# Moving the half-column products of a two-layer graph kernel next to its 64-unit tiles, on one Trainium2 core

## The chip, the cores and the metric

The kernel runs on one core of a Trainium2 chip. The metric is the device time of one launch in microseconds (us), as the median of several executions. A second kind of number comes from one profiled execution, in which the hardware records every instruction; its time is told beside the timed ones.

The engines are named as in the profile: PE is TensorE (matrix products; PEld its weight loads), DVE is VectorE, ACT is ScalarE, POOL is GpSimd, SP is the engine whose queue issues nearly all DMAs. Each works through its own instructions in order and waits on semaphores for the others.

## The reference

There are 128 graphs of 128 nodes with 64 features. Layer 0 sums, for each node j, a small network over its neighbours k (those with `adj > 0`); layer 1 is a weighted sum over neighbours and a linear map. Both are applied to a normalised, rectified x and added to x:

```
h = max(layernorm(x), 0)
A = h @ W1a + h @ W1b + b1          # per node j; W1 is (128, 192): two halves of 64 rows
C = h @ W1b                         # per node k
hm[j] = sum over k with adj[j,k] > 0 of relu(A[j] - C[k])      # 192 hidden units
x1 = x + hm @ W2 + deg * b2         # W2 is (192, 64)
h2 = max(layernorm(x1), 0)
out = x1 + (adj @ h2) @ W.T
```

Everything is float32 in and out. A node has some 15 neighbours, so the kernel does not evaluate all 128 x 128 pairs.

## The kernel before, in words

**Groups.** The 128 graphs are taken in 32 groups of four (`G = 4`). A group's neighbours are put into slots: each node's neighbours are ranked within four quarters of the nodes, six slots to a quarter (`D = 6`), and the rare rest goes through "edges" (`et`, `R`, `S2`, `X`). `S` is a one-hot matrix of slots, computed on VectorE; `ca` holds the projections A and C split into three bfloat16 parts. `S` and `ca` are restacked by DMA into `S3` and `k3` (12 DMAs each, all on SP's queue, lines 442 to 640), so that one product with 96 rows picks a slot's neighbour exactly and a second adds the node's own part.

**Jobs.** A group's main work is 24 jobs (`Job`, line 818). Each fills a two-bank PSUM tile, of which there are three (`gtile`), and drains it. Hidden units 0 to 127 are one kind: products that use all 128 columns of TensorE, drained by a VectorE reduction (`hm<-g`). Hidden units 128 to 191 are the other: 64 units, so two graphs share a tile, each with 64 of TensorE's columns (shapes `96*64` in the profile), drained by a ScalarE activation into `T` and additions on GpSimd. I call the second kind 64-unit jobs. `ORDER` (line 920) puts them in runs of two: positions 4 and 5, 10 and 11, 16 and 17, 22 and 23 of 24.

**Pieces.** Between the jobs stand pieces of work for other groups. While group g's jobs run, `AHEAD` (line 890) prepares group g+1 and `BEHIND` (line 909) finishes group g-1; a key t means "after job t", and at one t the order is `OWN`, `BEHIND`, `AHEAD` (`pieces`, line 927). The pieces that matter here, with their tiles in PSUM (two small ones, `mtile`, used in turn):

- `pre_adj`, `pre_norm`, `pre_hT` (tiles `pt`, `ph`): transposes of adjacency and of normalised x, and the neighbour mask `maskT`.
- `pre_rank` (line 442, tile `pq`): the ranks, one product with 512 columns, copied by ScalarE to `qs`; VectorE makes `ov` and then the slots `S` from it (`pre_slots`).
- `pre_count` (tile `pd`), `pre_proj` (tiles `pp`, of the large kind), `pre_stack` (the DMAs of `k3`), `pre_edge_a` (line 623, tile `pv`; VectorE makes `mid`, ScalarE the first `et`), `pre_edge_b`, `pre_place`, `pre_edge_c`, `pre_edge_d` (tiles `pj`, `prt`, `pgq`).
- `edge_sum` (tile `pe0`) and `edge_sum1` (line 731, tile `pe1`): the edges' part for the first 128 and the last 64 units. In the profile both are called `pe`. VectorE makes `u0` and `u1` from them. `pe1` is two all-column transposes and then four half-column products.
- `post0` (line 751, tile `py`): y = u W2, as two half-column products with `u0` (`w2h`) and one all-column product with `u1` (`w2bd`), added up in PSUM; ScalarE copies it to `ys`.
- `post1` (line 772, tile `pty`): transposes of `ys` back; VectorE adds to `x1` and takes the statistics. `post2`: a square root on ScalarE (`sdb`), two small VectorE operations (`rsb`, `mrb`), then four ScalarE activations `h2` (in the profile `h<-x,mrb,rsb`). `post3` (line 791, tile `pga`): four half-column products with `h2`; `post4` (tile `po`): the last linear map, and the store.

**What sets the order.** TensorE's instructions keep the order in which the program writes them (`mm`, line 180). The other engines' orders within the main loop are free: a planner in the tile layer decides them when the kernel is built, and which PSUM buffer a tile gets. So a piece that is moved can change the order on VectorE, ScalarE and GpSimd well beyond its own place.

Group 0 and the last group have orders of their own (`ORDER0`, `ORDERL`); after the last group its `BEHIND` pieces run alone.

Of the kernel before, what the change touches and what calls it, by code (L numbers as in the profile page):

```python
# [150 lines left out]
def kernel(  # L151
# [28 lines left out]
    def mm(*args, **kw):  # L180
        return tc.keep_in_program_order(nc.tensor.matmul(*args, **kw))  # L181
# [23 lines left out]
    B, N, F = x.shape  # L205
# [22 lines left out]
    with ExitStack() as main:  # L228
# [11 lines left out]
        def mtile(name):  # L240
            return ps_m.tile([P, 512], F32, tag="m", name=name)
# [7 lines left out]
        w2bd = const.tile([P, 2, O], F32, tag="w2bd", name="w2bd")  # L249
# [134 lines left out]
        def bc(t, n, axis):  # L384
            shape = list(t.shape)
            shape.insert(axis, n)
            return t.unsqueeze(axis).to_broadcast(shape)
# [67 lines left out]
        def pre_slots(g, first, last):  # L455

            d = groups[g]
            if first == 0:
                d["S"] = one.tile([P, D, G * N], BF16, tag="S", name=f"S{g}")
            n = last - first  # L460
            vec.tensor_tensor(
                d["S"][:, first:last], bc(d["qs"].rearrange("k b j -> k (b j)"), n, 1),
                rks[:, first:last], ALU.is_equal,
            )
            if last < D:
                return
            d["S3"] = grp.tile([K3, Q, D, G * N], BF16, tag="S3", name=f"S3{g}")
            for q in range(Q):
                for part in range(3):
                    sp.dma_start(  # L470
                        d["S3"][part * QN : (part + 1) * QN, q],
                        d["S"][q * QN : (q + 1) * QN],
                    )
# [277 lines left out]
        def post0(g):  # L751
            d = groups[g]
            py = mtile(f"py{g}")
            d["py"] = py
            for p in range(2):
                s = slice(p * O, (p + 1) * O)
                mm(
                    py[s, 0 : 2 * N], w2h,
                    d["u0"][:, 2 * p : 2 * p + 2].rearrange("h r j -> h (r j)"),
                    start=True, stop=False, skip_group_check=True,  # L760
                )
            w = w2bd.rearrange("h p o -> h (p o)")
            mm(
                py[:, 0 : 2 * N], w, d["u1"].rearrange("h r j -> h (r j)"),
                start=False, stop=True, skip_group_check=True,
            )
            d["ys"] = tmp.tile([P, 2, N], F32, tag="ys", name=f"ys{g}", bufs=1)
            act.activation(
                d["ys"].rearrange("p r j -> p (r j)"), py[:, 0 : 2 * N], AF.Copy
            )  # L770
# [47 lines left out]
        class Job:  # L818
# [70 lines left out]

        AHEAD = {  # L890
            0: (pre_adj,),
            2: (pre_norm, pre_hT,),
            3: (pre_rank, lambda g: pre_slots(g, 0, 2),),
            4: (lambda g: pre_slots(g, 2, 4),),
            5: (pre_count,),
            6: (lambda g: pre_slots(g, 4, D),),
            7: (lambda g: pre_proj(g, 0),),
            9: (pre_edge_a,),
            12: (lambda g: pre_proj(g, 1), pre_stack,),
            19: (pre_edge_b,),  # L900
            20: (pre_place,),
# [7 lines left out]
        BEHIND = {  # L909
            0: (slot_sum,),  # L910
            1: (edge_sum,),
            4: (edge_sum1,),
            8: (post0,),
            10: (post1,),
            15: (post2,),
            16: (post3,),
            19: (post4,),
        }

# [114 lines left out]
```

## Time and profile before

| | before |
|---|---|
| timed executions | 993.23, 994.23, 1002.85 us, median 994.23 |
| profiled execution | 1005.13 us |
| its span, first to last instruction | 1003.4 us |
| mean granted TensorE clock | 0.978 |
| busy: PE, DVE, ACT, POOL | 94%, 80%, 70%, 76% |
| VectorE's waits for TensorE (`hm` for `g`) | 113.2 us, 113 times |
| TensorE's waits for `k<-ca` | 18.5 us, 22 times, the longest 7.2 |
| TensorE's waits for `hm` | 15.2 us, 31 times |

The profiled execution was slower than two of the three timed ones, so differences are formed within the profile and then set against the median. The busy share of PE counts pipelined products by modelled ends; where products follow each other closely, the distance between their starts is the better measure of what each costs. A group's mean in the table of costliest groups mixes shapes where it says "+2 forms". The waits name the instruction that released a wait; a wait that hides behind another engine's longer one costs nothing.

### The profile page before, as it was taken

What the parts mean: (1) busy time and instruction counts of PE and PEld (TensorE: products, weight loads), DVE (VectorE), ACT (ScalarE), POOL (GpSimd) and SP (SyncE); (2) the same over time, 40 slices, a digit from 0 to 9 for tenths busy, and PEclk for the clock granted to TensorE, in tenths of its full rate; (3) what the DMA queues carried; (4) which work ended last, traced back from release to release, by engine and by line L of the source; (5) the groups of instructions that cost most, each with busy time, mean ns of one, the idle gap of its engine ahead of it and who ended that gap; (6) DMA issues with size and microseconds to landing.
All of it is one profiled execution on the core that took longest, in us unless ns stands there. A gap on an engine that the chain in (4) does not pass through costs nothing.

```text
span 1003.4 us, 26630 instructions
## 1 busy us (share of the span) xinstructions
PE 947.9 (94%) x9994; PEld 695.8 (69%) x9994; DVE 801.2 (80%) x1769; ACT 706.3 (70%) x1732; POOL 767.5 (76%) x1134
## 2 busy tenths in 40 slices
PE   3899999999999999999999999999999999999996
PEld 2577776677776777777677767677767777777674
DVE  7677888877888878788887787887888887788863
ACT  5557876667877767787677785677787677787652
POOL 3287877787877878877788786778877788787783
PEclk9599999999999999999999999999999999999997
DMA  3626665556766555766555765555766655665520
GB/s 87 134 69 160 153 139 131 127 121 150 157 138 139 129 122 136 164 143 142 126 125 126 159 148 123 124 126 136 164 141 138 134 127 124 157 148 127 111 60 13
DMA packets 88293, 129.89 MB, mean 129 GB/s; under 512 B 47200, under 2 KB 63968, under 8 KB 88160
## 3 DMA queue, kind: packets, MB, share of 16 engines
q1 hardware_dynamic: 87584, 127.98, 56.4%
q8 instruction: 80, 1.31, 0.5%
q14 instruction: 53, 0.43, 0.1%
q10 hardware_dynamic: 576, 0.16, 0.1%
HBM read 13.01 MB, written 4.19 MB: 17 GB/s over the span
## 4 chain that ended last, share of the span: by engine, by line
PE 37%; DVE 23%; ACT 19%; DMA 7%; POOL 6%; issue 4%; SPq 3%; DVEq 0%; POOLq 0%; ACTq 0%
PE g L181 21%; DVE hm L198 7%; DVE S L198 7%; PE pe L181 7%; DMA k<-ca 6%; ACT ca L198 5%; ACT et L198 4%; POOL T L198 4%; SPq L198 3%; ACT h L198 3%; ACT T L198 3%; DVE u L198 3%; POOL ca L198 2%; ACT z L198 2%; PE px L181 2%
## 5 line engine op out<-in xcount | busy, mean ns | idle before, releaser
L198 POOL TENSOR_TENSOR T<-T 128x192 f32<-128x192 f32 (+2 forms) x768 | 545.7, 717 | 124.3 <-ACT T L198 84.4
L198 DVE TENSOR_REDUCE hm<-g 128x64 f32<-128x768 f32 x512 | 473.4, 950 | 117.0 <-PE g L181 113.2
L181 PEld LDWEIGHTS <-k 96*128 96x128 bf16 (+1 forms) x6144 | 412.8, 104 | 213.9 <-issue 87.0
L181 PE MATMUL g<-S,k 96*128 96x384 bf16 (+1 forms) x2048 | 392.5, 333 | 34.9 <-DMA k<-ca 18.5
L181 PE MATMUL g<-id,k 96*128 96x192 bf16 (+1 forms) x4096 | 383.9, 248 | 0.0
L198 ACT ACTIVATE T<-g 128x768 f32<-128x768 f32 x256 | 210.2, 823 | 51.7 <-PE g L181 45.7
L198 POOL TENSOR_TENSOR ca<-rest,ca 128x384 bf16<-128x384 f32 x126 | 113.9, 924 | 85.3 <-ACT ca L198 83.6
L198 ACT ACTIVATE ca<-pp 128x768 bf16<-128x768 f32 x64 | 51.4, 804 | 63.7 <-PE pp L181 63.7
L198 DVE TENSOR_TENSOR S<-qs,rks 128x1024 bf16<-128x1024 bf16 x93 | 86.8, 934 | 0.0
L198 ACT ACTIVATE hT<-ph 128x256 f32<-128x256 f32 x32 | 12.3, 384 | 89.4 <-PE ph L184 89.4
L181 PE MATMUL pe<-RT,X 128*64 128x128 f32 (+1 forms) x512 | 71.3, 282 | 0.0
L181 PE MATMUL pp<-wp,hT 64*128 64x448 f32 x256 | 68.5, 613 | 0.0
L198 ACT ACTIVATE z<-pp,ns 128x128 f32<-128x128 f32 (+1 forms) x256 | 66.0, 348 | 0.0
L198 DVE TENSOR_TENSOR rest<-pp,ca 128x768 f32<-128x768 f32 x64 | 60.7, 949 | 3.0 <-ACT ca L198 2.8
L198 ACT ACTIVATE ca<-rest 128x768 bf16<-128x768 f32 x64 | 55.2, 862 | 9.3 <-DVE rest L198 9.2
L181 PEld LDWEIGHTS pe<-RT,X 128*64 128x64 f32 (+1 forms) x512 | 53.4, 166 | 5.3 <-issue 5.3
L198 ACT ACTIVATE et<-et,half 128x128 f32<-128x128 f32 x128 | 56.8, 449 | 0.0
L181 PE MATMUL px<-ca,S 128*128 128x192 bf16 x384 | 52.7, 246 | 0.0
L181 PE MATMUL px<-ca,R 128*128 128x192 bf16 x384 | 52.6, 246 | 0.0
L198 ACT ACTIVATE h<-x,mrb,rsb 128x64 f32<-128x64 f32 x128 | 51.6, 479 | 0.8 <-DVE mrb L198 0.8
L181 PE MATMUL pe<-ident,z 128*128 128x128 f32 x192 | 49.9, 287 | 0.0
L198 ACT ACTIVATE h<-x,mra,rsa 128x64 f32<-128x64 f32 x128 | 48.7, 432 | 1.1 <-DVE mra L198 1.1
(128 smaller groups left out, 1203.9 us busy)
## 6 DMA issues: line engine op xcount, KB each, us to landing
S<-S SPq DMA_DIRECT2D x372, 192.0 KB, 4.0
k<-ca SPq DMA_DIRECT2D x384, 96.0 KB, 2.2
adj<-in_adj_dram SPq DMA_DIRECT2D x32, 256.0 KB, 3.1
x<-in_x_dram SPq DMA_DIRECT2D x32, 128.0 KB, 2.7
out_dram<-ot SPq DMA_DIRECT2D x32, 128.0 KB, 2.2
w<-in_L_gnn_W_dram SPq DMA_DIRECT2D x2, 96.0 KB, 4.4
bias<-in_L_gnn_b_dram ACTq DMA_DIRECT2D x1, 96.0 KB, 3.8
w2a<-in_L_gnn_W_dram ACTq DMA_DIRECT2D x1, 32.0 KB, 2.1
```

The lines of the kernel that those rows point to most:

```text
L181: return tc.keep_in_program_order(nc.tensor.matmul(*args, **kw))
L198: ins = f(*args, **kw)
```

## The change

Four pieces move to an earlier place (`edge_sum1`, `pre_rank`, `pre_edge_a`, `post2`), three to a later one (`post0`, `post1`, `post3`), and the products of `post0` change their order: the all-column product opens the sum in PSUM, and the two half-column products close it. The pieces' arithmetic is otherwise the same. After the change, `edge_sum1` ends in its half-column products directly before job 4, `post0` in its own directly before job 10, `post3` stands directly behind job 17, and nothing stands between the two jobs of any run.

```
         def post0(g):
...
-            for p in range(2):
-                s = slice(p * O, (p + 1) * O)
-                mm(
-                    py[s, 0 : 2 * N], w2h,
-                    d["u0"][:, 2 * p : 2 * p + 2].rearrange("h r j -> h (r j)"),
-                    start=True, stop=False, skip_group_check=True,
-                )
             w = w2bd.rearrange("h p o -> h (p o)")
             mm(
                 py[:, 0 : 2 * N], w, d["u1"].rearrange("h r j -> h (r j)"),
-                start=False, stop=True, skip_group_check=True,
-            )
+                start=True, stop=False, skip_group_check=True,
+            )
+            for p in range(2):
+                s = slice(p * O, (p + 1) * O)
+                mm(
+                    py[s, 0 : 2 * N], w2h,
+                    d["u0"][:, 2 * p : 2 * p + 2].rearrange("h r j -> h (r j)"),
+                    start=False, stop=True, skip_group_check=True,
+                )
...
         AHEAD = {
             0: (pre_adj,),
-            2: (pre_norm, pre_hT,),
-            3: (pre_rank, lambda g: pre_slots(g, 0, 2),),
+            2: (pre_norm, pre_hT, pre_rank),
+            3: (lambda g: pre_slots(g, 0, 2),),
...
-            9: (pre_edge_a,),
+            8: (pre_edge_a,),
...
         BEHIND = {
             0: (slot_sum,),
             1: (edge_sum,),
-            4: (edge_sum1,),
-            8: (post0,),
-            10: (post1,),
-            15: (post2,),
-            16: (post3,),
+            3: (edge_sum1,),
+            9: (post0,),
+            13: (post1,),
+            14: (post2,),
+            17: (post3,),
             19: (post4,),
         }
```

More of the change, by code (lines that the diff above doesn't have):

```diff
@@ L754, in post0 @@
             d["py"] = py
+            w = w2bd.rearrange("h p o -> h (p o)")
+            mm(
+                py[:, 0 : 2 * N], w, d["u1"].rearrange("h r j -> h (r j)"),
+                start=True, stop=False, skip_group_check=True,
+            )
             for p in range(2):
@@ L759, in post0 @@
                     d["u0"][:, 2 * p : 2 * p + 2].rearrange("h r j -> h (r j)"),
-                    start=True, stop=False, skip_group_check=True,
+                    start=False, stop=True, skip_group_check=True,
                 )
-            w = w2bd.rearrange("h p o -> h (p o)")
-            mm(
-                py[:, 0 : 2 * N], w, d["u1"].rearrange("h r j -> h (r j)"),
-                start=False, stop=True, skip_group_check=True,
-            )
             d["ys"] = tmp.tile([P, 2, N], F32, tag="ys", name=f"ys{g}", bufs=1)
```

## The prediction

> **What bounds the kernel now.** I read the busy shares first, then the waits, then one group of four graphs instruction by instruction: group 9 of the 32, from the end of its `pe0` products (394.91 us) to the end of the next group's (425.05 us). All clock times below are this group's unless I say otherwise.
>
> ```profile
> PE 947.9 (94%) x9994; PEld 695.8 (69%) x9994; DVE 801.2 (80%) x1769; ACT 706.3 (70%) x1732; POOL 767.5 (76%) x1134
> ```
>
> TensorE looks like the only bound, but a share is an average. In the stretches the picture is different; first TensorE's timeline (start, length, what, and in brackets the idle time and who ended it):
>
> ```profile
> 396.36 0.39 PE L181 MATMUL pq<-maskT,triq 128*128 128x512 bf16 x1
> ...
> 397.02 0.50 PE L181 MATMUL g<-id,k 96*64 96x192 bf16 x8
> 397.45 0.44 PE L181 MATMUL pe<-ident,z 128*128 128x128 f32 x2
> 397.82 0.66 PE L181 MATMUL pe<-RT,X 128*64 128x128 f32 x8
> ...
> 402.36 0.48 PE L181 MATMUL g<-S,k 96*128 96x384 bf16 x2 [0.55 <-DVE hm L198]
> ...
> 413.19 0.50 PE L181 MATMUL g<-id,k 96*64 96x192 bf16 x8
> 413.52 0.61 PE L181 MATMUL pga<-adjT,h 128*64 128x128 f32 x8
> ...
> 421.04 0.32 PE L181 MATMUL g<-S,k 96*128 96x384 bf16 x1 [0.22 <-DMA k<-ca]
> ```
>
> Two things are to be seen. First the price of changing between half columns (the `96*64`, `128*64` shapes) and all columns (`128*128`): the same eight half-column products take 397.02 to 397.45, 0.43 us, when all-column work follows, and 413.19 to 413.52, 0.33 us, when half-column work (`pga`) follows. One change costs 0.10 us (0.095 between single records, in all 30 groups). Second, TensorE stands still twice in the group: at job 8 for VectorE, at jobs 0 and 1 for the DMAs of `k3`. VectorE ahead of job 8:
>
> ```profile
> 395.63 0.67 DVE L198 TENSOR_TENSOR u<-hs,pe 128x512 f32<-128x512 f32 x1
> 396.22 1.81 DVE L198 TENSOR_REDUCE hm<-g 128x64 f32<-128x768 f32 x2
> 397.95 0.28 DVE L198 TENSOR_SCALAR ov<-qs 128x512 bf16<-128x512 bf16 x1
> ```
>
> From `maskT` (395.02, just after `pe0`) VectorE works without a gap to the reduction that frees job 8's PSUM buffer (402.32), so that stretch is VectorE's length, not TensorE's. The chain of waits (start, length, what) closes the loop at the other end:
>
> ```profile
> 420.04 2.27 DMA k<-ca
> ...
> 422.36 0.67 PE g L181 x5
> ```
>
> SP issues 24 stacking DMAs back to back from the last slot operation (401.26) to 420.64; the last lands at 422.31 and job 1 waits for it. So there are two loops of nearly one length: by TensorE about 29.25 us (29.1 in groups without a `k3` wait), by SP and DMA the rest, mean 29.8 over 29 groups. The 0.55 between them is TensorE's wait for `k3`.
>
> **The change, part by part.** The built program has 576 changes of column or row mode before and 398 after, six fewer in each full group; at 0.095 that is 0.57 us a group, 17 us in all, if TensorE's time were the kernel's.
>
> *Two of the six go with `edge_sum1` (position 4 to 3): 0.19 us, worth nothing.* They lie between `pe0` and job 8, where TensorE waits 0.55 for VectorE; the wait grows instead.
>
> *The other four go with `post0` (products swapped, position 9 instead of 8, so its halves meet job 10) and `post1` (10 to 13): about 0.35 us.* (One replaced change stood behind the tiny `pv` products and cost 0.065.) They lie between job 8 and the group's end, which is TensorE's. `post1`'s own transposes (0.28) only change place. Gains here would end at the next `k3` wait unless SP is faster too; no DMA is moved or removed.
>
> *`pre_rank` (3 to 2) adds a wait.* `pq` now follows `ph` directly. TensorE reaches it at 395.63, but `pq`'s buffer was `pe0`'s and is freed by `u0` on VectorE at 396.30. TensorE stands 0.7 us, covered by job 8's wait (0.55 + 0.19; were that cover gone, 0.7 a group). `pq` thus starts when it did before, ScalarE's `qs` ends at about 397.4 as before, but on VectorE `ov` now stands after one reduction instead of two: ready at 397.2, it waits 0.2. Everything behind it, job 8's release and the slots that SP waits for, comes 0.2 us later. Bounds 0 to 0.3.
>
> *`pre_edge_a` (9 to 8), `post2` (15 to 14), `post3` (16 to 17): the step that decides.* `post1` is three positions later, `post3` one later, so the chain transposes, `x1`, statistics, square root, `h2`, `pga` has four jobs instead of six. And the planner put ScalarE's work in another order: in the built program the four `h2` come behind the drain of job 16. ScalarE before:
>
> ```profile
> 410.98 0.81 ACT L198 ACTIVATE h<-x,mrb,rsb 128x64 f32<-128x64 f32 x2
> ...
> 412.06 0.82 ACT L198 ACTIVATE h<-x,mrb,rsb 128x64 f32<-128x64 f32 x2
> ...
> 413.46 0.59 ACT L198 ACTIVATE X<-px 128x256 f32<-128x256 f32 x2
> ...
> 414.17 0.87 ACT L198 ACTIVATE T<-g 128x768 f32<-128x768 f32 x1
> 414.86 0.45 ACT L198 ACTIVATE agg<-pga 128x256 f32<-128x256 f32 x1
> ```
>
> `h2` was done at 412.88, 0.64 us ahead of `pga`. Now I walk the new order with the steps (start to next start) of these rows. Job 8 starts at 402.56, its reduction and `mid` end at 404.55; then ScalarE: `et` x4 1.18, `ys` 0.30, T 0.71, `ca` 0.74, T 0.72, `et` x4 1.16, `ca` 0.69, z x4 0.89, `e` x2 0.40, R 0.66, X x2 0.42, `ca` 0.74, X 0.26, root 0.19, X 0.16, job 16's T 0.71: 414.48. Each input is ready when its turn comes (closest: the second `rest` at 412.3, `mr` at 414.33). Four `h2` at 0.33: 414.96 to 415.95. TensorE: job 8 to job 16 took 10.49 before, now 10.49 - 0.35, so job 16 starts at 412.70 and job 17 ends at 414.02. There `pga` waits for the first `h2`, then the third, then the last at 415.95; its last product and the change of mode take 0.3, and job 18 starts at 416.3 instead of 414.72: **1.58 us later**. The stall inside it is about 1.8 us. From below, the order alone demands 1.3: job 16's T cannot start before job 16 ends, and 0.17 + 0.71 + 1.46 must pass before the last `h2` is there, against 1.0 in which TensorE gets to that product. From above I take 2.2, if ScalarE gets to T 0.4 later. Behind it wait all of TensorE, ScalarE's `agg`, `po`, `ot`, the store and the next load on SP, which has room.
>
> *`k3` then comes early enough.* It lands 0.2 later (422.5), but TensorE asks for that part at about 423.5, so the old wait of 0.55 a group is gone.
>
> **Sum.** 1.58 - 0.55 = 1.0 us a group, 30 groups: 30 us; the bounds (stall 1.3 with no `ov` wait, 2.2 with 0.3) give 0.4 to 1.6 a group, 12 to 48. The shorter last group and the swap in the tail, where nothing covers the halves, are worth a few tenths each way. The profiled execution took 1005.13 us with a span of 1003.4; one group in it (574 to 607) took 33.1, which a late DMA and a clock drop explain. I add to the median of 994.23 and leave 1 us for intervals where the old wait was already above the mean: **1023 us**.
>
> **Rivals.**
>
> *The clock drops at the new stall.* The windows of that one slow group, with TensorE's busy time in the second column and the granted clock behind the five engines:
>
> ```profile
> 600.36:603.78 3.42, 1.31 (x12) 0.91 (x11) 1.00 (x2) 1.56 (x5) 3.26 (x5) 1.00 0.40 98
> 603.78:607.20 3.42, 3.42 (x24) 3.16 (x22) 0.83 (x1) 0.00 (x0) 1.31 (x4) 0.50 0.20 58
> ```
>
> After 3.41 us with TensorE busy for 1.31 the clock was halved for one such stretch; after a stretch with 2.44 (from 928.02) it was not, after one with 1.93 (from 44.00) it was. A whole new stall in one stretch leaves about 2.2: undecided. If it counts, some 12 groups would hold it whole, at 1.5 us (what that group lost beyond its 2.1 us wait): 18 us more, 1041. The Trainium skill (TensorE: Matmul & The Clock Gate, Part 1 and "Why this matters for your kernels") has the clock fall only after a wholly idle window of some 3.4 us and calls gaps up to about 3 us safe, by which this rival would cost nothing; the drop above came after a window that was one third busy, so the trace speaks against leaning on that.
>
> *Wait for wait.* If the stall comes out near its lower bound and SP's loop near its upper spread (27.4 us from `pe0` to the last landing in this group), the `pga` wait only takes the place of the `k3` wait: within 10 us of now, 994 to 1004. For it: the margin is a half microsecond a group.
>
> *Faster.* ScalarE reaches `h2` before job 17 ends (before 414.0), and the DMAs speed up with TensorE, so that the 0.35 to 0.57 us count: 977 to 984. It decides only if ScalarE's run gains 1.9 us; the order of job 16's drain ahead of `h2` speaks against it.
>
> That the change doesn't do what it says is out: the mode changes are gone from the built program.
>
> **How the numbers follow.** Forecast 0.60 (1006 to 1034, stall and `ov` wait within bounds), clock 0.18 (1035 to 1050), wait for wait 0.16 (994 to 1004), faster 0.06. The range 1000 to 1045 leaves out the faster case, some 0.08 of wait for wait and 0.04 above. One per cent, 10 us, is about what a measurement can tell from no change: slower 0.77, same 0.17, faster 0.06.
>
> **What would show it.** After: TensorE idle before `pga`, released by ScalarE `h`, 1 us and more in nearly every group, 30 to 55 us in all; waits of TensorE for `k<-ca` nearly gone; a wait of `pq` for VectorE's `u`; about 30.8 us from `pe0` to `pe0`; job 8 still waiting for `hm`. Wrong if `pga` hardly waits, if the `k3` wait stays, or if half-clock stretches appear in many groups.

## The result and the profile after

The changed kernel takes 1058.51 us, median of 6 runs (1057.65 to 1060.13). The kernel before, run beside it, takes 996.29 us (median of 6). The ratio is **1.062, 95% interval 1.058 to 1.065**: slower by some 62 us. Forecast were 29 us and a range up to 1045. The direction held, the amount was more than twice the forecast, and the time lies outside the range.

The profiled executions differ by 55 us in span (1058.4 and 1003.4). Summed from one group's end of the `pe0` products to the next, 30 times, they differ by 57.7 us (955.1 and 897.3). The traces differ by less than the times because the traced execution of the kernel before was a long one (1005.13 us, median 996.29), with one group of 33.11 us in it. I work with the 57.7.

The busy shares of the changed kernel are the first thing that the page shows:

```profile
PE 957.6 (90%) x9994; PEld 710.9 (67%) x9994; DVE 825.7 (78%) x1769; ACT 705.2 (67%) x1732; POOL 757.1 (72%) x1134
```

Every engine's share fell, so somebody waits. And VectorE is busy for 24.5 us longer than before (801.2) with the same 1769 instructions, so some of its instructions have become longer. By tile these are `mr` (15.9 us more in all 32 groups) and its counterpart in the first normalisation, `mra` (13.9 us more); in the profile `mr` is called `mrb`. The view of TensorE's waits says for whom (engine, tile, line, releaser; then us in total, times, longest):

```profile
PE pga L181 <- ACT h L198: 51.2, 61, 2.7
...
PE g L181 <- DVE hm L198: 14.1, 31, 0.7
...
PE pq L181 <- DVE u L198: 10.1, 30, 1.1
...
PE g L181 <- DMA k<-ca: 6.5, 1, 6.5
```

`pga` now waits for `h2` in every group, 51.2 us in all. The wait for `k3` is gone but for the one at the start, job 8 still waits for VectorE, and `pq` waits for `u0`: four of the five signs that the prediction named. The fifth, a period of about 30.8 us, did not come: 18 of the 30 groups take 31.28 to 31.56 us, two take 30.79, and every third or so takes 32.95.

TensorE's timeline in the group that begins at 415.11 us (the end of its `pe0`; columns: start, length, what, and in brackets the idle time before it and who ended it):

```profile
416.29 0.39 PE L181 MATMUL pq<-maskT,triq 128*128 128x512 bf16 x1 [0.31 <-DVE u L198]
...
422.57 0.48 PE L181 MATMUL g<-S,k 96*128 96x384 bf16 x2 [0.44 <-DVE hm L198]
...
433.64 0.50 PE L181 MATMUL g<-id,k 96*64 96x192 bf16 x8
435.55 0.43 PE L181 MATMUL pga<-adjT,h 128*64 128x128 f32 x2 [1.42 <-ACT h L198]
436.22 0.76 PE L181 MATMUL pga<-adjT,h 128*64 128x128 f32 x6 [0.23 <-ACT h L198]
436.91 0.50 PE L181 MATMUL g<-S,k 96*128 96x384 bf16 x2
```

Job 17 ends at about 433.97, and then TensorE stands 1.42 and 0.23 us before job 18 starts at 436.91, which is 21.80 after the end of `pe0`. Before the change it was 19.81 (414.72 - 394.91). So job 18 comes 1.99 us later, where the prediction had 1.58. ScalarE's timeline shows how the `h2` were reached:

```profile
433.55 0.29 ACT L198 ACTIVATE sdb<-mvb,eps 128x4 f32<-128x4 f32 x1
433.74 0.26 ACT L198 ACTIVATE X<-px 128x128 f32<-128x128 f32 x1
433.90 0.81 ACT L198 ACTIVATE T<-g 128x768 f32<-128x768 f32 x1
435.06 1.43 ACT L198 ACTIVATE h<-x,mrb,rsb 128x64 f32<-128x64 f32 x4 [0.36 <-DVE mrb L198]
```

The order is the one that the walk had: root, X, the drain of job 16, then four `h2`. The drain hands over at 434.61, 19.50 after `pe0`; the walk said 19.57. But `h2` does not start there. ScalarE stands idle for 0.36 until VectorE has made `mr`, and `h2` starts at 435.06, 19.95 after `pe0`. VectorE's timeline, with `ov` as well, for which the prediction showed the row before the change:

```profile
417.35 0.29 DVE L198 TENSOR_SCALAR ov<-qs 128x512 bf16<-128x512 bf16 x1 [0.25 <-ACT qs L198]
...
434.05 0.17 DVE L198 RECIPROCAL rsb<-sdb 128x4 f32<-128x4 f32 x1
434.14 0.20 DVE L198 BATCH_NORM_STATS2 sta<-x 128x6 f32<-128x64 f32 x1
434.25 0.77 DVE L198 SCALAR_TENSOR_TENSOR mrb<-mvb,rsb 128x4 f32<-128x4 f32 x1
```

`ov` waits 0.25 (forecast 0.2). `mr` works on four numbers per partition, and before the change it took 0.18 us (median of 32). Here it takes 0.77. GpSimd's timeline has what lies beside it, two additions in a row:

```profile
434.09 1.78 POOL L198 TENSOR_TENSOR ca<-rest,ca 128x384 bf16<-128x384 f32 x2
```

The first of these two additions takes 0.91 us and starts 0.16 us ahead of `mr`, and `mr` ends 0.02 us after that addition does. So it is in 28 of the 32 groups, in which `mr` takes over 0.5 us. In two groups `mr` starts just ahead of this addition, and there it takes 0.16 us (VectorE, then GpSimd):

```profile
179.49 0.16 DVE L198 SCALAR_TENSOR_TENSOR mrb<-mvb,rsb 128x4 f32<-128x4 f32 x1
```

```profile
179.51 1.79 POOL L198 TENSOR_TENSOR ca<-rest,ca 128x384 bf16<-128x384 f32 x2
```

These two are the groups of 30.79 us. In the kernel before `mr` isn't alone either. In group 9 of before (VectorE, then GpSimd):

```profile
409.25 0.17 DVE L198 SCALAR_TENSOR_TENSOR mrb<-mvb,rsb 128x4 f32<-128x4 f32 x1
```

```profile
408.81 0.59 POOL L198 TENSOR_TENSOR T<-T 128x192 f32<-128x192 f32 x1
```

There too `mr` ends 0.02 us after a GpSimd addition, in 31 of 32 groups, but it comes only 0.16 us (median) ahead of that addition's end. The Trainium skill has a rule for this (SBUF — State Buffer, "Who interferes with whom"): a VectorE instruction with two inputs in SBUF contends with a GpSimd instruction that reads SBUF, because its second input comes through a port that the two share, which the page calls an exclusive lock. `mr` has two inputs in SBUF, the addition reads two, and the trace agrees: an `mr` that starts during an addition ends 0.02 us after it, unless its own 0.16 us last longer.

The second loss is in the granted clock. In the clock record of the changed kernel the stretches at half clock between start and tail are 3.41 us long and start whole multiples of 3.41 us apart; stretches on this grid are called windows here. First column the stretch, then its length, the busy times of PE, PEld, DVE, ACT and POOL with their counts, then the granted clock:

```profile
401.22:404.63 3.41, 1.78 (x14) 1.11 (x15) 1.54 (x10) 3.04 (x8) 3.33 (x5) 0.99 0.60 156
404.63:408.04 3.41, 3.41 (x19) 2.61 (x17) 2.29 (x3) 0.08 (x1) 3.10 (x6) 0.51 0.67 159
...
623.07:626.48 3.41, 2.08 (x32) 1.51 (x30) 3.41 (x18) 3.04 (x10) 3.23 (x6) 1.00 0.80 198
626.48:629.90 3.42, 3.09 (x26) 2.21 (x27) 1.33 (x6) 2.19 (x7) 3.26 (x5) 1.00 0.69 161
```

Where the whole stall falls into one window, TensorE is busy for 1.78 us of it, and the next window runs at half clock. Where the stall is split between two windows, 2.08 are left and nothing happens. Ten stretches of 3.41 us at half clock lie in the middle of the run, in every third or fourth group. Each costs 32.95 - 31.29 = 1.66 us, together 16.6 (two of them lie in the first and the last of the 30 groups, which have other lengths). The regularity is an accident of lengths: two plain groups and one slow one are 95.5 us, close to 28 windows (95.6), so the stall comes back to the same place in the window.

### The profile page after: what moved, and what is told of

The parts are those of the page before. It is cut to its first block, busy times and chain, and to the rows that moved or that the text cites. A ratio compares the mean times of both kernels' runs of the same rounds, so it can differ in the third digit from the quotient of the medians.

```text
span 1058.4 us, 26630 instructions
## 1 busy us (share of the span) xinstructions
PE 957.6 (90%) x9994; PEld 710.9 (67%) x9994; DVE 825.7 (78%) x1769; ACT 705.2 (67%) x1732; POOL 757.1 (72%) x1134
## 4 chain that ended last, share of the span: by engine, by line
PE 38%; DVE 31%; ACT 26%; issue 2%; POOL 1%; DVEq 0%; ACTq 0%; POOLq 0%
PE g L181 21%; DVE hm L198 9%; DVE S L198 8%; ACT et L198 7%; PE pe L181 6%; ACT T L198 5%; ACT ca L198 5%; ACT h L198 3%; ACT z L198 3%; DVE rest L198 3%; PE pga L181 2%; DVE u L198 2%; DVE mrb L198 2%; PE po L181 2%; ACT qs L198 2%
## 5 line engine op out<-in xcount | busy, mean ns | idle before, releaser
L198 POOL TENSOR_TENSOR T<-T 128x192 f32<-128x192 f32 (+2 forms) x768 | 535.6, 703 | 229.9 <-ACT T L198 187.8
L198 DVE TENSOR_REDUCE hm<-g 128x64 f32<-128x768 f32 x512 | 479.6, 950 | 151.9 <-PE g L181 143.2
L181 PEld LDWEIGHTS <-k 96*128 96x128 bf16 (+1 forms) x6144 | 422.8, 105 | 187.5 <-issue 72.9
L181 PE MATMUL g<-id,k 96*128 96x192 bf16 (+1 forms) x4096 | 389.4, 249 | 0.0
L198 ACT ACTIVATE T<-g 128x768 f32<-128x768 f32 x256 | 202.6, 805 | 66.2 <-PE g L181 66.1
L181 PE MATMUL pga<-adjT,h 128*64 128x128 f32 x256 | 38.3, 302 | 51.2 <-ACT h L198 51.2
L198 ACT ACTIVATE qj<-pj 128x512 bf16<-128x512 f32 x32 | 19.1, 597 | 88.4 <-PE pj L181 88.2
L198 POOL TENSOR_TENSOR hs<-hm 128x256 f32<-128x256 f32 x64 | 46.3, 726 | 29.5 <-DVE rsa L198 27.4
L181 PEld LDWEIGHTS pga<-adjT,h 128*64 128x64 f32 x256 | 18.8, 137 | 69.8 <-ACT h L198 65.6
L198 ACT ACTIVATE h<-x,mrb,rsb 128x64 f32<-128x64 f32 x128 | 45.9, 430 | 10.9 <-DVE mrb L198 10.8
```

The lines of the kernel that those rows point to most:

```text
L198: ins = f(*args, **kw)
```

## The experiments

Each run was timed beside the kernel before again, whose median was 999 to 1002 us; the ratios are to that. Theory A, from the prediction, is that the late chain `post1`, `post2`, `h2`, `pga` is the loss, and that the saved mode changes are worth nothing. From the trace I added the two surcharges, the held `mr` (B) and the half clock (C). The rival was that the planner's other orders on VectorE, ScalarE and GpSimd cost the time wherever `post1` stands.

### post1 put back (e1_post1_back)

```
+            10: (post1,),
+            15: (post2,),
+            16: (post3,),
-            13: (post1,),
-            14: (post2,),
-            17: (post3,),
```

> The changed kernel with post1, post2 and post3 at their old positions 10, 15 and 16; everything else as changed. Theory 1 (the loss is TensorE's wait for h2 ahead of pga, some 2.0 us in each group, and the half-clock stretches that it sets off): pga no longer waits, the period is the DMA loop's 29.8 us and the 0.2 us of the slots' delay, 994 to 1004 us. Rival (the loss comes from pre_rank, pre_edge_a and post0, whose new places lengthen VectorE's stretch ahead of job 8): it stays above 1030.

It took 1024.44 us, ratio 1.025 (1.021 to 1.029): between the two. `pga` waits only at the start, there is no half-clock stretch between start and tail, and a group takes 30.68 us on the mean (29.91 before, 31.84 in the changed kernel). So three fifths of the loss go when the chain is put back. The waits of this kernel name what costs the rest:

```profile
PE pq L181 <- DVE u L198: 11.7, 30, 1.1
PE prt L181 <- DVE ot L198: 11.0, 29, 0.4
PE pty L184 <- ACT ys L198: 8.2, 31, 0.5
...
ACT h L198 <- DVE mra L198: 17.6, 31, 0.6
```

The planner had put the first normalisation's four `h` ahead of `qj` on ScalarE, and there they wait 0.58 us a group for `mra`, the other small multiplication of this kind, which was held in its turn (0.99 us; 0.21 before). New, small waits of TensorE follow: `prt` 0.38, `pty` 0.27. Of these waits the changed kernel has only the one of `pq` (10.1 us). So what is left here isn't simply a part of the changed kernel's loss: with `post1` put back the planner made another order, which has costs of its own.

### post1 moved late, alone (e2_post1_late_alone)

The kernel before, with only `post1` at 13, `post2` at 14 and `post3` at 17.

> The kernel before with post1, post2 and post3 alone at positions 13, 14 and 17. Theory 1: 29.25 us of TensorE's own path, 0.19 less for two drains, 2.0 more for the wait ahead of pga, and half-clock stretches in some groups: 1040 to 1056 us. Rival: within 1% of before.

It took 1044.76 us, ratio 1.045 (1.041 to 1.049), as expected. One of TensorE's waits carries it:

```profile
PE pga L181 <- ACT h L198: 46.5, 61, 2.7
```

Most groups take 30.97 us, and seven windows in the middle of the run are at half clock. So the late chain alone makes some seven tenths of the loss (0.045 of 0.062), half clock included. With the 0.025 of the first experiment that is more than the whole, so the two parts don't simply add up. `mr` takes 0.30 us here and `h2` doesn't wait for it, yet TensorE idles 1.46 us ahead of `pga` (1.65 in the changed kernel, medians), and the clock falls all the same.

### Products that fill the stall (e3_fill)

Ahead of `pga`, twelve pairs of half-column products go into unused columns of its PSUM tile. Nothing reads them; they only keep TensorE busy while it waits for `h2`.

```
         def post3(g):
...
+            for n in range(12):
+                for p in range(2):
+                    mm(
+                        pg[p * F : (p + 1) * F, 2 * N : 4 * N], oneb[:, 0:F],
+                        trib.unsqueeze(1).to_broadcast([P, 2, P]),
+                        start=True, stop=True, skip_group_check=True,
+                    )
```

> The changed kernel with 12 pairs of idle half-column products (256 columns each, some 0.11 us a pair, 1.3 us in all, into unused columns of pga's PSUM tile) ahead of pga in each group: more work for TensorE, none of it on the chain to h2. If the half-clock stretches come from the idle time ahead of pga, they vanish and the base period of 31.28 us stays: 10 times 1.66 us less, 1038 to 1045. If they come from something else, the time stays at 1055 to 1062; if the filler delays pga, it is longer.

It took 1053.20 us, ratio 1.054 (1.050 to 1.058), in none of the expected ranges. All half-clock stretches between start and tail are gone, so it is the idle TensorE that halves the clock. But the time fell by only 5 us, because the groups became longer, 31.66 us. Two waits, both of this kernel, tell that its other orders differ too:

```profile
PE pq L181 <- DVE u L198: 16.6, 30, 1.1
...
ACT h L198 <- DVE mra L198: 25.7, 31, 0.9
```

`pq` waits 16.6 us where it waited 10.1, and `h` waits 0.83 us a group for `mra`. So the run shows that C is caused by the stall; the size of C is better taken from the trace of the changed kernel (ten times 1.66).

### h2 ahead of the drain on ScalarE (e4_h2_first)

An order edge on ScalarE alone: job 16's drain comes behind the four `h2`.

> The changed kernel with ScalarE's order alone changed: the four h2 stand ahead of job 16's drain T. By the walk of the prediction (ScalarE's queue decides when h2 starts) h2 comes 0.71 us earlier, some 21 us less, and without the half-clock stretches about 1020. By the trace after (h2 waits 0.36 us for mr on VectorE, which ends with GpSimd's addition) h2 starts no earlier: 1052 to 1062.

It took 1065.03 us, ratio 1.066 (1.061 to 1.070), above both expectations and 6 us more than the changed kernel. ScalarE's waits show why nothing was gained:

```profile
ACT h L198 <- DVE mrb L198: 31.3, 31, 1.1
```

The place on ScalarE is now free, `h2` waits there for `mr`, about 1 us a group (0.36 before the edge), and ends 21.47 us after `pe0` on the mean instead of 21.38. Groups without half clock take 31.3 or 31.6 us, and twelve stretches are at half clock instead of ten. Part of the prediction's step falls here. The drain of job 16 ahead of `h2` is how ScalarE's time was filled, but what sets the time of `h2` in the changed kernel is `mr`.

### mr without a second SBUF input (e5_mr_scalars)

```
-            vec.scalar_tensor_tensor(mr, mv[:, :, 0], -1.0, rs, ALU.mult, ALU.mult)
+            for b in range(G):
+                vec.tensor_scalar(
+                    mr[:, b : b + 1], mv[:, b, 0:1], rs[:, b : b + 1], -1.0, ALU.mult, ALU.mult
+                )
```

One instruction with two streamed inputs becomes four with one streamed input and one scalar per partition each.

> The changed kernel with mr (the shift of the normalisation) made by four one-column operations with one streamed SBUF input each, in place of one operation with two. If the 0.77 us of mr in the trace after is a hold by GpSimd's addition, which two SBUF inputs meet and one does not, mr ends some 0.4 us earlier, h2 follows job 16's drain directly: 0.36 us a group, 11 us, and with the stall shorter the half-clock stretches go or become fewer: 1031 to 1050. If one input is held as well, or if ScalarE's queue decides: 1055 to 1062.

It took 1029.78 us, ratio 1.030 (1.025 to 1.034), a little below the expected 1031 to 1050: 29 us less than the changed kernel, from one line. The timelines of this kernel, in a group whose `pe0` ended at 403.49; first VectorE:

```profile
422.64 0.58 DVE L198 TENSOR_SCALAR mrb<-mvb,rsb 128x1 f32<-128x1 f32 x4
```

GpSimd:

```profile
422.50 1.77 POOL L198 TENSOR_TENSOR ca<-rest,ca 128x384 bf16<-128x384 f32 x2
```

ScalarE:

```profile
422.27 0.81 ACT L198 ACTIVATE T<-g 128x768 f32<-128x768 f32 x1
422.96 1.43 ACT L198 ACTIVATE h<-x,mrb,rsb 128x64 f32<-128x64 f32 x4
```

GpSimd's additions lie beside `mr` as they did, and `mr` is no longer held: each of the four small operations takes 0.2 us, and the first `h2` needs only the first of them. `h2` starts when the drain hands over (422.96, 19.47 after `pe0`; forecast 19.57). Job 18 starts 1.51 us later than before the change (forecast 1.58), and a group takes 30.79 us (forecast about 30.8). TensorE still idles 1.15 us a group ahead of `pga`, but the half-clock stretches between start and tail are gone; the windows in which the stall lies whole look like this:

```profile
144.64:148.05 3.41, 2.26 (x27) 1.27 (x22) 2.13 (x14) 3.41 (x11) 3.41 (x5) 1.00 0.71 189
148.05:151.47 3.42, 3.42 (x36) 2.89 (x34) 2.90 (x4) 0.98 (x3) 3.10 (x6) 1.00 0.68 157
```

So the loss splits into three terms. What is left with `mr` repaired, the forecast's mechanism, is 924.6 - 897.3 = 27.3 us over the 30 groups. The hold itself is 31.29 - 30.79 = 0.5 a group in the 28 groups that have it, 14 us. The half clock, which goes with the hold, is 16.6 us. The sum is 57.9; the traces differ by 57.7.

### post1 one position earlier (e6_post1_at_12)

The changed kernel with `post1` at 12 and `post2` at 13.

> The changed kernel with post1 at position 12 and post2 at 13, post3 still at 17: the chain to h2 starts some 1.7 us earlier, but in the built order mr still stands behind the reduction of job 15. If the position of post1 decides, the wait ahead of pga nearly goes: 1000 to 1015. If the orders on VectorE and ScalarE decide (mr behind that reduction, and held by GpSimd's addition): 1045 to 1060.

It took 1020.14 us, ratio 1.020 (1.015 to 1.025), between the two expectations. `pga` still waits in every group, two fifths as long as in the changed kernel:

```profile
PE pga L181 <- ACT h L198: 20.6, 60, 2.7
```

Between start and tail the clock is never halved, and a group takes 30.53 us. `mr` is held here too (0.56 us, this time beside GpSimd's `e<-e,x`). So one position is worth about 0.8 us a group in a chain that is late, and one position was not enough.

### pre_rank and edge_sum1 early, alone (e7_rank_early_alone)

The kernel before, with only `pre_rank` at 2 and `edge_sum1` at 3.

> The kernel before with edge_sum1 at 3 and pre_rank at 2 alone, two drains fewer in each group. By the prediction these drains are worth nothing (job 8 waits for VectorE anyway) and ov's wait for qs delays the slots by 0.2 us: 0 to 8 us longer. If the drains counted: 5 us shorter.

It took 1013.43 us, ratio 1.013 (1.009 to 1.017): 13 us more, where I had expected 8 at the most. Its waits:

```profile
PE g L181 <- DMA k<-ca: 16.1, 20, 6.4
PE g L181 <- DVE hm L198: 13.6, 30, 0.7
PE pq L181 <- DVE u L198: 13.3, 30, 0.7
```

The last slot operation ends 6.50 us after `pe0` on the mean instead of 6.24, so SP's 24 DMAs start 0.26 later, and the wait for `k3` stays. The loop through the DMAs moves with it: 30.15 us a group against 29.91, 7 us by the trace. The rest of the 13 fits the choice of the traced executions: this run's is its fastest (1009.76 us), the one of the kernel before was a long one (1005.13). In the changed kernel this delay is hidden, because `pga` is later than `k3`; for a repair it counts.

### post1 back and mr repaired (e8_post1_back_mr)

The first experiment with `mr` as four operations.

> The changed kernel with post1, post2, post3 back at 10, 15, 16 (as in the earlier run with post1 back) and mr taken as four small VectorE operations, each with one operand streamed from SBUF and the others as per-partition scalars. If what kept that earlier run at 30.61 us a group was the held mr, which blocked ScalarE for 0.58 us a group ahead of job 18, the period falls to 29.9 to 30.2 us and the time to 1002 to 1012. If it was ScalarE's order alone (four h2 ahead of qj, whether or not they wait), the period stays above 30.4: 1018 to 1027.

It took 1018.27 us, ratio 1.016 (1.011 to 1.020), a group 30.50 us, the second of the two expectations: most of what the first experiment left isn't the hold. That it is ScalarE's order and `pre_rank` is argued from the waits, not shown by a run. The waits `pq` (12.5 us), `pty` (8.2) and `prt` (7.9) are still there; `pre_rank` and `edge_sum1` alone made a group 0.24 us longer; here it is 0.59.

### Mode changes saved, costs taken out (e9_drains_kept, e12_drains_kept_r_later)

What is left of the change when both costs go: `pre_rank` and `edge_sum1` at their old places, `post0` with its swapped products at 9, `pre_edge_a` at 8, `post1` at 11, `post2` at 13, `post3` at 17, and `mr` as four operations. Of the 576 changes of mode 456 remain (398 in the changed kernel).

> What is left of the change when both costs are taken out and four of the six mode changes stay saved: pre_rank and edge_sum1 at their old places (3 and 4), post0 with its swapped products at 9, pre_edge_a at 8, post1 at 11, post2 at 13, post3 at 17, mr as four small operations. If the mode changes only lengthen the wait for the stacking DMAs, as the prediction says, no gain: 990 to 1000, waits of TensorE for k<-ca of 15 us and more. If TensorE's time is the kernel's, 0.38 us a group is saved: 980 to 988. If a later post1 costs in itself, even with h2 early, 1005 or more.

It took 1003.49 us, ratio 1.002 (0.999 to 1.004): no difference that can be told. The group takes 30.07 us. That there is no gain was expected; where it goes was not, as the waits show:

```profile
PE g L181 <- DVE hm L198: 14.1, 31, 0.9
PE g L181 <- ACT T L198: 10.6, 31, 0.8
PE g L181 <- DMA k<-ca: 8.5, 6, 6.8
PE po L181 <- ACT agg L198: 5.2, 30, 0.5
```

Of the waits for `k3` hardly one is left besides the start. In their place TensorE waits 0.34 us a group for ScalarE's drain of job 16, which the planner had put behind `R`, and 0.17 for `agg`. The next run takes that away by two order edges on ScalarE:

```
+            if g and "drained" in groups[g - 1]:
+                tc.add_manual_dep(
+                    ins.ins, groups[g - 1]["drained"].ins.name,
...
+                if behind is not None:
+                    tc.add_manual_dep(
+                        ins.ins, behind.ins.name,
```

The first edge puts `R` behind the drain of job 17, the second `h` behind `RT`.

> The run with four of the six mode changes saved and both costs taken out, with two edges more in ScalarE's order: R of the next group only behind the drain of job 17, and the four h of the group after it only behind RT, as in the kernel before. In the run without these edges TensorE waited 0.34 us a group for job 16's drain (which stood behind R) and 0.17 for agg. If these waits were where the saved mode changes went, the period falls from 30.06 towards 29.5 us: 983 to 994. If the stacking DMAs set the end once TensorE is faster, the waits of TensorE for k<-ca come back (15 us and more) and the time stays at 995 to 1003.

It took 999.66 us, ratio 1.000 (0.998 to 1.002). The wait for the drain is gone, the one for `agg` isn't (5.2 us as before the edges):

```profile
PE g L181 <- DVE hm L198: 16.1, 31, 0.9
PE g L181 <- DMA k<-ca: 10.6, 11, 6.6
```

A group takes 29.84 us against 29.91. The `k3` waits came back in part (4.0 us without the start, 11.3 before), and four mode changes fewer, 0.35 us, show up as less than 0.1, which the one group of 33.11 us in the trace of before would explain alone. In one group that I set beside one of before, job 18 starts 0.12 us sooner after job 8. The products on the way are 0.35 shorter, but TensorE pauses 0.26 at job 15 and later 0.16 ahead of `po`. What releases job 15 the trace does not name.

### Two stacking DMAs on ScalarE's queue (e10_drains_and_queue, e11_queue_alone)

To shorten SP's chain, the last two of the 24 DMAs go out from ScalarE's queue, once in the kernel of e9_drains_kept and once in the kernel before.

```
-            for part, q in order:
-                sp.dma_start(
+            for n, (part, q) in enumerate(order):
+                (act if n >= 10 and g else sp).dma_start(
```

> The same, and the last two stacking DMAs of k3 of each group go out from ScalarE's queue, so that SP's chain of 24 issues is shorter by some 1.2 us. If SP's chain and TensorE's work are two loops of nearly one length, this is the first kernel in which the saved mode changes count: period 28.9 to 29.4 us, 968 to 986. If ScalarE pays for the issues (0.4 to 0.5 us each) on its way to qj, or if VectorE ahead of job 8 is the bound, 990 or more.

> The kernel before, with only the last two stacking DMAs of k3 on ScalarE's queue. If SP's chain is the longer loop, the waits of TensorE for k<-ca go and the period falls from 29.8 to 29.2 to 29.4 us: 978 to 988; the distance to the run with the mode changes saved as well is then their worth, up to 0.38 us a group, 11 us. If TensorE or VectorE is the bound anyway, within 5 us of before.

They took 1149.33 us (ratio 1.147, 1.142 to 1.151) and 1195.03 us (1.194, 1.189 to 1.198). Both are far longer than was expected, and both fail as tests of what a shorter SP chain is worth, but the second tells something by itself. The queues of SP and ScalarE in it:

```profile
409.32 12.55 SPq L198 DMA_DIRECT2D k<-ca  x10
```

```profile
413.11 1.16 ACTq L198 DMA_DIRECT2D k<-ca  x2
```

SP needs 12.55 us for ten issues, where it needed 9.17 for twelve. It stands still from 410.19, after its first one, to 415.25: 2.14 us after ScalarE's first issue, which is the usual time to landing (2.1). In the trace these DMAs take one of eight completion counters (semaphores) in turn, and each waits until the last DMA with the same counter has landed. ScalarE's two have the counters behind that of SP's first, but ScalarE comes to them late: its first lands at 415.24, and SP's second, on the same counter, goes out at 415.25. So SP waits for a DMA that isn't its own (39 such waits for `k<-ca`, 166.1 us). The last part of `k3` lands 3 us later (29.97 us after `pe0` on the mean, 27.02 before), TensorE stands for a whole window, and the clock follows:

```profile
419.49:422.90 3.41, 0.09 (x1) 0.09 (x1) 0.44 (x1) 1.30 (x3) 3.17 (x6) 0.99 0.68 159
422.90:426.31 3.41, 3.21 (x15) 2.20 (x16) 0.96 (x1) 0.60 (x1) 1.21 (x3) 0.50 0.35 81
```

No version here beats the kernel before.

## Why the prediction was wrong, and where it was right

**The failed term is `mr`, taken as ready at 414.33.** In "the step that decides" the walk took each input of ScalarE as ready when its turn came, and named `mr`, 0.15 us ahead of the end of the drain, as the closest. That rested on `mr` being as short as in its old place, where it was short because it came 0.16 us ahead of the end of a GpSimd addition. Three positions later it comes near the start of GpSimd's `ca<-rest,ca`, takes 0.77 us, and `h2` starts 19.95 us after `pe0` instead of 19.50. Job 18 came 1.99 us later instead of 1.58. In the prediction's own measure the stall is that and the 0.41 by which job 16 now starts sooner: 2.40, where the prediction had about 1.8 (1.58 + 0.35 = 1.93 by the same sum) with bounds of 1.3 and 2.2; with `mr` repaired it is 1.9. The upper bound looked at ScalarE alone ("if ScalarE gets to T 0.4 later"); what GpSimd does at that time was not asked.

**The clock rival was sized rightly and given too small a chance.** It was to cost 18 us (12 groups at 1.5), and it cost 16.6 (10 at 1.66). Its point of decision was also near: the forecast stall would leave TensorE busy for "about 2.2" of a window, which the prediction called undecided. With that stall (`mr` repaired) 2.26 are left and the clock holds; with the held `mr` 1.78 are left and it falls, so that a sign of being wrong that the prediction had named, half-clock stretches in many groups, came true. In the changed kernel one small error thus paid twice: 14 us by itself and 16.6 through the clock. A held `mr` is not the only way there: with `post1` late alone `h2` didn't wait for `mr`, and the clock fell in seven windows. The rival laid the clock on the middle of the forecast (1041). No case laid it on a stall at the upper bound, although a longer stall is what makes a fall likely: 48 + 18 is 66 us, and 62 were measured.

**What held.**

- The late chain as a cause: 27.3 us are left when `mr` is repaired, forecast 30 (29 in the median); that run's ratio, 1.030, has 1023 us (1.029 of 994.23) in its interval.
- The drain of job 16 hands over at 19.50 after `pe0`, forecast 19.57; the period without the surcharges is 30.79, forecast about 30.8.
- The wait for `k3` is gone, job 8 still waits for `hm` (0.44), `pq` waits for `u0`, `ov` 0.25 for `qs` (forecast 0.2).
- The mode changes are worth nothing that can be measured: with both costs out, ratios 1.002 and 1.000. The reason was only half right. The gain does not stop at the `k3` wait alone; it turns into several waits of 0.1 to 0.3 us for ScalarE and others.

**What was understated.** With `pre_rank` at 2 the slots end 0.12 us later in the changed kernel (forecast 0.2, bounds 0 to 0.3), and the last part of `k3` lands no later (26.83 us after `pe0` on the mean, 27.02 before). But with `pre_rank` and `edge_sum1` moved alone it is 0.26, and where the DMAs set the end this costs 7 us by the trace and 13 by the times. That ScalarE's order decides when `h2` starts was too narrow: with `h2` put first on ScalarE nothing came sooner, for `mr` was the limit.

## What to carry to other kernels

When a piece is moved, check what the other engines do at its new time, and not only the queue that it moves in: a tiny VectorE operation with two SBUF inputs can be held for nearly the whole of a GpSimd addition (here 0.77 us, the addition 0.91), and a form with per-partition scalars avoids it. Price a new stall together with the clock, by how much of a 3.41 us window it leaves busy, and at the stall's upper bound too. In this kernel, saving 0.1 us here and there on one engine of a kernel whose four engines are each busy for 70 to 94% of the time mostly made small waits elsewhere, so a move must first be shown not to lengthen any chain.

## What the runs showed of the hardware

- **The clock falls well before a window is idle.** In the changed kernel and the runs with `post1` late alone and `h2` first, windows in which TensorE was busy for 1.76 to 2.00 of 3.41 us were followed by half clock; with 2.08 (changed kernel) and 2.26 (`mr` repaired) the clock held. Busy time alone doesn't draw the line: in the run of e10_drains_and_queue the clock held behind five windows with 1.82 to 1.95. The largest that fell is from the run with `h2` first, the smallest that held from e10_drains_and_queue:

```profile
564.76:568.17 3.41, 2.00 (x16) 1.25 (x17) 1.32 (x8) 2.72 (x6) 2.02 (x3) 1.00 0.64 160
568.17:571.58 3.41, 3.41 (x20) 2.78 (x19) 2.39 (x4) 0.56 (x3) 3.18 (x5) 0.50 0.65 149
```

```profile
171.55:174.96 3.41, 1.82 (x15) 1.41 (x16) 0.81 (x1) 0.37 (x1) 3.10 (x6) 1.00 0.60 138
174.96:178.37 3.41, 3.41 (x40) 3.08 (x38) 2.14 (x5) 0.46 (x2) 0.52 (x2) 1.00 0.28 77
```

  The Trainium skill (TensorE: Matmul & The Clock Gate, Part 1) asks for a wholly idle window; a stall of 1.42 and 0.23 us was enough here, and the measurement decides. That a filled stall keeps the clock agrees with the page.
- **A [128 x 4] operation with two SBUF inputs that starts during a GpSimd operation ends with it**, some 0.02 us later, unless its own 0.16 us last longer. So it does in the kernel before too: it took 0.18 us in one place and 0.77 in another, and `mra` 0.21 and 0.99 (in the run with `post1` back). Started 0.02 us ahead of the addition it took 0.16. With one streamed input, beside the same GpSimd addition, it was not held.
- **A halved clock can lock in** where groups and windows have a common multiple: 28 windows are 95.6 us, three groups 95.5.
- **A DMA on another queue can stop SP** through the completion counters that they take in turn: for 5 us in the group shown.
